# An RWKV and Hadamard FFN kernel on one core: the order of the next tokens' statistics and the next weights' loads in the first block's last product

## Chip, core and metric

The kernel runs on one core of a Trainium2 chip. The metric is the device time in microseconds from launch to end; several runs of each kernel are taken and their median is compared. One further execution was recorded by the hardware profiler; all start times below are counted from the first instruction of that recording.

## What is computed

The input `x` has 4 sequences of 2048 tokens with 512 channels, all in float32. After a layer norm without gain or bias, two branches are added to the input: an RWKV-v4 attention and a gated FFN with a Walsh-Hadamard transform of its hidden layer.

```python
xn = _layernorm(x, axis=-1)
# attention branch
shifted = jnp.pad(xn, ((0, 0), (1, 0), (0, 0)))[:, :-1]
xr, xk, xv = (mu * xn + (1.0 - mu) * shifted for mu in (mu_r, mu_k, mu_v))
r, k, v = xr @ Wr.T, xk @ Wk.T, xv @ Wv.T
attn = (sigmoid(r) * wkv_v4(k, v, wkv_w, wkv_u)) @ Wo.T     # a recurrence over the tokens
# FFN branch
hidden = fwht(silu(xn @ W1.T) * (xn @ W3.T))                # 2048 wide
out = x + attn + hidden @ W2.T
```

## The kernel before

The 8192 tokens are worked through in 8 blocks of `TB` = 1024, two blocks to a sequence. A block has these stages: the three projections to r, k and v; 16 products up (`up`, gate and linear weights together) with the recurrence woven in; and a last product, called down, in which the hidden layer and the recurrence's output are multiplied by the joined weights of `W2` (with the Hadamard transform folded in) and `Wo`. The products are Strassen-like: seven products of sums and differences ("forms") of quarters stand for eight. Forms of weights are made once, on POOL, in the block that uses them first (`seven_forms`, four additions), and then kept in DRAM (`part_w`, `down_w`, `deep_w`) for later blocks.

Block 0 does its down product in `down_whole` (line 636), one level deep: seven products of four pieces each. A piece is 320 KB of weights; it serves ten matmuls of 128x512. `pieces_w` is a ring of eight pieces. `Down.product` (line 613) first issues the load of the piece seven ahead and then its own matmuls, so the load stands in SyncE's queue at the place where the code reaches it, and it waits until the piece that had its slot has been used. Later blocks use `down` (line 727), with another hand-written order.

Work for the next block is spread into the down product by an object of the class `Chores` (line 931) and a function `next_parts` (line 1063):

- `chores.start()` copies the last column of the old tokens on DVE and issues the load of the next block's tokens by channel, 2 MB into `xnT`, on SyncE.
- `chores.statistics(n)` advances the generator `statistics` (line 163) by n steps. For eight groups of tokens, ACT sums over the channels (into `sums`); POOL makes `mean` of it; eight more ACT passes make the sums of squares; three POOL instructions make `rs` (the inverse deviation, and the mean times it). SyncE stores `rs` to `stat_d` in DRAM and loads it back to all partitions as `spread`, a part of the tile `v_sb`. In block 0 all 16 steps are issued at once. The token-major input of these passes, `x_tok`, lies in the tile `tf`; its load (`load_tokens`) is issued before the down product begins.
- `chores.tokens(n)` advances the normalizing on DVE (it reads `spread` and `xnT`) and the token forms.
- `next_parts()` issues the loads of the first two weight tiles of the next block, into the three-tile ring `ring_a` (tile name `part`). At the end of block 0, the first has its forms already and is loaded whole from `part_w` (896 KB). The second is the first of the projections' weights, used for the first time in block 1: it is loaded from `wpart` (512 KB), and `load_parts` (line 394) at once issues its four form additions on POOL.

All engines are wrapped in `InOrder`: each engine, and each engine's queue of DMA issues, keeps the order in which the code issues. All DMAs are issued on SyncE. So an instruction that waits on SyncE or POOL holds up whatever stands behind it on that engine. (The profile gives almost every instruction the line of this wrapper, L35; so instructions are told apart by the names of their tiles.)

In `down_whole`, product 0 (pieces 0 to 3 of 28) is issued first, then the differences of the right side for a later product, then the next block's work, and then product 1 with `c11`, which adds to the residual x11 and stores it; the loads of pieces 11 to 14 are issued in product 1.

Of the kernel before, what the change touches and what calls it, by code (L numbers as in the profile page):

```python
# [18 lines left out]
TP = TB // P  # L19
# [21 lines left out]
def tile_rwkv_attn_hadamard_ffn(  # L41
# [73 lines left out]
    def bank():  # L115
        turn[0] += 1
        return banks[(turn[0] - 1) % 8]
# [276 lines left out]
    def load_parts(i, n):  # L394
        t = ring_a.tile([P, 7, KH, P], F32, tag="a", name=f"part_{i}_{n}")
        if is_first(i, n):
            sp.dma_start(out=t[:, 0:4], in_=wpart[n])
            forms_in(t)
        else:
            sp.dma_start(out=t, in_=part_w[n])  # L400
        return t
# [179 lines left out]
    def parts_of(kh, half):  # L581

        return [quarter(kh, half, rh, cols) for rh in range(2) for cols in (lo, hi)]
# [4 lines left out]
    def differences(out, x0, x1):  # L588
        for o, p0, p1 in zip(out, x0, x1):
            difference(o, p0, p1)  # L590

    def add(slot, pt, cols=whole):
        dve.tensor_tensor(slot[:, cols], pt[:, cols], slot[:, cols], ALU.add)
# [42 lines left out]
    def down_whole(i, chores, next_parts):  # L636

        d = Down(i)
        y11, y12, y21, y22 = (parts_of(kh, half) for kh in range(2) for half in range(2))
        pa, pb, pc = ([bank() for _ in range(KH)] for _ in range(3))  # L640
        s5 = [small.tile([P, H], F32, tag="s5", name=f"s5_{i}_d{g}") for g in range(KH)]
        d.residual(x11, 0, 0)
        d.plain_product(0, pa, (0, 0), lambda g: act.copy(pb[g], pa[g]), True)
        differences(y11, y12, y11)
        chores.start()
        next_parts()
        chores.statistics(2 * TP)

        def c11(g):
            add(x11[g], pa[g])  # L650
            d.store(x11[g], 0, g, 0)

        d.plain_product(1, pa, (1, 0), c11)
        d.residual(x12, 0, 1)
        d.residual(x22, 1, 1)
        d.plain_product(4, pc, (0, 0), lambda g: act.copy(s5[g], pc[g]), True)
        differences(y12, y22, y12)
        for g in range(KH):
            add(x22[g], s5[g])
        chores.tokens(6)  # L660
        d.plain_product(6, pc, (1, 1), lambda g: None)
        differences(y22, y22, y11)
        d.plain_product(5, pb, (1, 1), lambda g: act.copy(u2_of[g], pb[g]))
        differences(y21, y21, y22)
        for g in range(KH):
            add(x12[g], pc[g])
            add(x12[g], u2_of[g])
            d.store(x12[g], 0, g, 1)
        d.residual(x21, 1, 0)
        chores.tokens(2)  # L670

        def c22(g):
            add(x22[g], pb[g])
            d.store(x22[g], 1, g, 1)

        d.plain_product(3, pb, (0, 1), c22)
        chores.tokens(4)
        chores.mix()

        def c21(g):  # L680
            add(x21[g], pb[g])
            d.store(x21[g], 1, g, 0)

        d.plain_product(2, pb, (1, 0), c21)
# [242 lines left out]
    def order_of(i):  # L927
        rkv, (first, *rest) = range(3 * KH), range(3 * KH, 3 * KH + NF)
        return [first, *rest] if i == 0 else [first, *rkv, *rest]
# [29 lines left out]
    for i in range(n_blocks):  # L959
# [46 lines left out]
        else:  # L1006


            def mix_chores(*kinds):
                for kind in kinds:  # L1010
                    mix_before(kind, 0)
                    for b in range(NB):
                        if b + 1 < NB:
                            mix_before(kind, b + 1)
                        mix_here(kind, b)
                        yield
                    yield from mix_forms(kind)
# [7 lines left out]
            chores, hooks = mix_chores(2, 0), [0]  # L1025
# [37 lines left out]
        def next_parts():  # L1063
            if not last:
                parts.extend(load_parts(i + 1, n) for n in order_of(i + 1)[:2])
# [3 lines left out]
        if i == 0:  # L1069
            down_whole(i, Chores(i + 1), next_parts)  # L1070
        else:
            down(i, Chores(i + 1), next_parts, last)
# [53 lines left out]
```

## Time and profile before

| | us |
|---|---|
| median of 3 runs (lowest, highest) | 3064.77 (3064.32, 3064.84) |
| the profiled execution's own time | 3062.49 |
| its span, first to last instruction | 3060.7 |
| TensorE (PE) busy in it | 3027.3 (99%) |
| VectorE (DVE) busy | 2471.0 (81%) |
| ScalarE (ACT) busy | 1014.1 (33%) |
| GpSimd (POOL) busy | 233.0 (8%) |

The mean granted TensorE clock was 0.997 of full speed, and the kernel moved 397.64 MB by DMA. Busy times overlap, since engines work beside each other, and ends of matmuls are modelled, so that a busy TensorE isn't always one at full rate. An arrow `<-` between two engines means that the left one waited for the right one; `out<-in` names the tiles of an instruction. PEld is the weight load on TensorE, SPq an issue of a DMA on SyncE.

The first block's down product stands between 310.21 us, where its first matmul starts, and 445.00 us, where the first matmul of block 1 starts. Seven more blocks follow in the span.

### The profile page before, as it was taken

The page shows a single profiled execution, that of the slowest core. Times are in us where ns is not written, and L with a number is a line of the kernel's source. Part 1 is how long each engine was busy: PE and PEld are TensorE (multiplying, and loading weights), DVE is VectorE, ACT ScalarE, POOL GpSimd, SP SyncE. Part 2 cuts the span into 40 slices and gives each one's busy share as a digit, 9 for nine tenths or more (in the row PEclk, how much of TensorE's full clock was granted, in tenths as well). Part 3 has the DMA queues.
Part 4 walks back from the last instruction along what each step waited for, and adds up shares of the span by engine and source line. Part 5 has one row for each costly group of instructions (what it writes and reads, how often), then busy time and mean ns, then how long its engine had stood idle before and what let it go on. Part 6 is the DMA issues. An engine that isn't in the chain of part 4 may idle for free.

```text
span 3060.7 us, 24403 instructions
## 1 busy us (share of the span) xinstructions
PE 3027.3 (99%) x8492; PEld 1615.3 (53%) x8492; DVE 2471.0 (81%) x2579; ACT 1014.1 (33%) x1822; POOL 233.0 (8%) x192
## 2 busy tenths in 40 slices
PE   8999899999999999999999999999999999999999
PEld 3444344446744476444764448544485444844458
DVE  5798548998878878888788888879798897988876
ACT  4233214333243332433234332333324333143321
POOL 3363002330000000000000000000000000000000
PEclk9999999999999999999999999999999999999999
DMA  4264424565522254222632226322352224522234
GB/s 174 74 200 172 173 69 146 202 216 190 177 75 82 90 211 141 73 84 78 230 134 72 76 102 223 125 73 72 147 190 107 83 72 164 180 97 84 72 119 146
DMA packets 136058, 397.64 MB, mean 130 GB/s; under 512 B 14336, under 2 KB 32768, under 8 KB 133760
## 3 DMA queue, kind: packets, MB, share of 16 engines
q1 hardware_dynamic: 135936, 396.09, 37.2%
q8 instruction: 68, 1.11, 0.1%
q14 instruction: 54, 0.44, 0.0%
HBM read 336.08 MB, written 59.96 MB: 129 GB/s over the span
## 4 chain that ended last, share of the span: by engine, by line
PE 86%; DVE 1%; DMA 1%; POOL 0%; ACT 0%; issue 0%; SPq 0%; DVEq 0%
PE bank L35 86%; DMA pieces_w<-deep_w 0%; DVE e1b L35 0%; POOL rs L35 0%; DVE right L35 0%; DMA pieces_w<-down_w 0%; DMA stat_d<-rs 0%; DVE sa L35 0%; DVE v_sb L35 0%; DVE e L35 0%; DVE bank L35 0%; DVE sb L35 0%; ACT tf L35 0%; SPq L35 0%; ACT s_d L35 0%
## 5 line engine op out<-in xcount | busy, mean ns | idle before, releaser
L35 PE MATMUL bank<-tf,part 128*128 128x512 f32 x2048 | 941.9, 592 | 0.0
L35 PE MATMUL bank<-right,pieces_w 128*128 128x256 f32 (+1 forms) x2928 | 792.5, 431 | 14.6 <-DMA pieces_w<-down_w 11.8
L35 ACT COPY bank<-bank 128x512 f32<-128x512 f32 (+1 forms) x638 | 337.1, 528 | 1413.7 <-PE bank L35 1377.5
L35 PE MATMUL bank<-xnT,part 128*128 128x512 f32 x1536 | 722.2, 593 | 1.2 <-DVE right L35 1.2
L35 PEld LDWEIGHTS bank<-right,pieces_w 128*128 128x128 f32 x2928 | 557.5, 191 | 242.9 <-issue 167.9
L35 PEld LDWEIGHTS bank<-tf,part 128*128 128x128 f32 x2048 | 389.6, 190 | 489.6 <-issue 461.8
L35 PEld LDWEIGHTS bank<-xnT,part 128*128 128x128 f32 x1536 | 292.0, 190 | 366.5 <-issue 358.9
L35 DVE TENSOR_TENSOR right<-right 128x1280 f32<-128x1280 f32 (+2 forms) x236 | 328.9, 1420 | 64.7 <-PE bank L35 63.7
L35 PE MATMUL bank<-right,part 128*128 128x512 f32 x840 | 369.6, 594 | 0.0
L35 DVE SCALAR_TENSOR_TENSOR right<-right,bank 128x512 f32<-128x512 f32 x256 | 174.7, 682 | 218.9 <-ACT right L35 218.6
L35 PEld LDWEIGHTS bank<-right,part 128*128 128x128 f32 x840 | 158.6, 190 | 203.0 <-issue 189.2
L35 ACT ACTIVATE right<-bank 128x512 f32<-128x512 f32 x308 | 183.8, 600 | 124.1 <-PE bank L35 105.9
L35 DVE RECIPROCAL e1b<-e1b 128x512 f32<-128x512 f32 x64 | 214.2, 3347 | 1.1
L35 DVE TENSOR_TENSOR bank<-bank,s 128x512 f32<-128x512 f32 x256 | 168.8, 691 | 37.3 <-ACT bank L35 23.7
L35 DVE TENSOR_TENSOR right<-right,bank 128x512 f32<-128x512 f32 x256 | 173.6, 678 | 11.5 <-PE bank L35 7.1
L35 POOL TENSOR_SCALAR mean<-sums 128x8 f32<-128x8 f32 x7 | 5.0, 715 | 1814.7 <-ACT tf L35 1462.7
L35 DVE SCALAR_TENSOR_TENSOR right<-xnT,vec,right 128x1024 f32<-128x1024 f32 x92 | 119.7, 1337 | 14.3 <-ACT right L35 14.3
L35 ACT COPY s<-bank 128x512 f32<-128x512 f32 x128 | 74.9, 585 | 144.9 <-PE bank L35 144.8
L35 POOL TENSOR_TENSOR part<-part 128x256 f32<-128x256 f32 x88 | 89.9, 1032 | 266.3 <-DMA part<-wpart 159.0
L35 ACT ACTIVATE right<-xnT,omm 128x1024 f32<-128x1024 f32 x92 | 100.3, 1143 | 12.3 <-PE bank L35 12.3
L35 PE MATMUL bank<-pieces_w,part 128*128 128x512 f32 x224 | 100.7, 592 | 0.0
L35 PE MATMUL bank<-k_sb,pieces_w 128*128 128x256 f32 x420 | 97.5, 379 | 0.0
(120 smaller groups left out, 2300.9 us busy)
## 6 DMA issues: line engine op xcount, KB each, us to landing
part<-part_w SPq DMA_DIRECT2D x148, 896.0 KB, 4.6
pieces_w<-deep_w SPq DMA_DIRECT2D x294, 320.0 KB, 3.1
pieces_w<-down_w SPq DMA_DIRECT2D x80, 320.0 KB, 5.4
part_w<-part SPq DMA_DIRECT2D x22, 896.0 KB, 6.1
tf<-x SPq DMA_DIRECT2D x7, 2048.0 KB, 7.9
xnT<-xT SPq DMA_DIRECT2D x7, 2048.0 KB, 10.0
deep_w<-pieces_w SPq DMA_DIRECT2D x6, 2240.0 KB, 8.1
v_sb<-xT SPq DMA_DIRECT2D x48, 256.0 KB, 8.1
```

The source lines that it names most:

```text
L35: return self.tc.keep_in_program_order(issue(*args, **kwargs))
```

## The change

In `down_whole` two lines change places:

```diff
         d.plain_product(0, pa, (0, 0), lambda g: act.copy(pb[g], pa[g]), True)
         differences(y11, y12, y11)
         chores.start()
+        chores.statistics(2 * TP)
         next_parts()
-        chores.statistics(2 * TP)
 
         def c11(g):
             add(x11[g], pa[g])
```

The statistics of the next block's tokens (16 ACT passes, four POOL instructions, the store of `rs` and the load of `spread`) are now issued ahead of the two weight loads and of the four form additions. The other blocks, which use `down`, are left as they were. What is computed stays the same.

## The prediction

> **What bounds the kernel now.** I read first the page's busy table and its costliest groups: TensorE is busy 3027.3 of 3060.7 us, at a mean granted clock of 0.997. Only time in which TensorE stands still or runs slowly can be won. TensorE's own waits are few, and the longest is one wait for a piece of the down weights:
>
> ```profile
> PE bank L35 <- DMA pieces_w<-down_w: 11.8, 1, 11.8
> PE bank L35 <- DMA right<-w: 9.9, 1, 9.9
> PE bank L35 <- ACT right L35: 3.9, 1, 3.9
> ```
>
> Columns: who waited for what, total us, times, longest. The timeline of TensorE puts it in the first block's last product, where the edit is; the table by stretches adds the clock (columns: busy us, matmuls, granted clock, DMA share, GB/s):
>
> ```profile
> 310.21 47.37 PE L35 MATMUL bank<-right,pieces_w 128*128 128x512 f32 x110
> 369.39 75.77 PE L35 MATMUL bank<-right,pieces_w 128*128 128x512 f32 x170 [11.81 <-DMA pieces_w<-down_w]
> 445.00 1.88 PE L35 MATMUL bank<-xnT,part 128*128 128x512 f32 x4
> ```
>
> ```profile
> 357.60:369.30 11.70, 0.00 (x0) 0.64 0.37 142
> 369.40:373.70 4.30, 4.30 (x5) 0.50 1.05 408
> ```
>
> See: 110 matmuls are 11 pieces of 10 (pieces 0 to 10), so what is late is piece 11; after the pause TensorE runs at half clock for a while. Why piece 11 is late is in SyncE's queue (start, issue time):
>
> ```profile
> 337.06 0.38 SPq L35 DMA_DIRECT2D xnT<-xT  x1
> 337.49 0.50 SPq L35 DMA_DIRECT2D part<-part_w  x1
> 338.04 0.42 SPq L35 DMA_DIRECT2D part<-wpart  x1
> 361.68 0.37 SPq L35 DMA_DIRECT2D stat_d<-rs  x1
> 363.24 0.32 SPq L35 DMA_DIRECT2D v_sb<-stat_d  x1
> 363.65 0.86 SPq L35 DMA_DIRECT2D pieces_w<-down_w  x2
> ```
>
> The queue stands for 23.1 us on the store of the statistics, and piece 11 is the first load behind it. POOL and ACT say what the statistics waited for:
>
> ```profile
> 348.03 5.33 POOL L35 TENSOR_TENSOR part<-part 128x256 f32<-128x256 f32 x4 [66.44 <-DMA part<-wpart]
> 353.33 0.24 POOL L35 TENSOR_SCALAR mean<-sums 128x8 f32<-128x8 f32 x1
> 359.43 0.20 POOL L35 TENSOR_SCALAR rs<-sums 128x8 f32<-128x8 f32 x1 [5.86 <-ACT tf L35]
> ```
>
> ```profile
> 332.88 0.19 ACT L35 ACTIVATION_READ_ACCUMULATOR tf<-tf 128x1 f32 x1
> 353.60 0.72 ACT L35 ACTIVATE tf<-tf,mean 128x512 f32<-128x512 f32 x1 [20.54 <-POOL mean L35]
> ```
>
> ACT's sums are done at 332.88+0.19 = 333.07. The mean on POOL stands in program order behind the four forms, which wait until 348.03 for their 512 KB from wpart. So ACT waits 20.54 us for a mean whose inputs were ready, and everything to piece 11 follows.
>
> **What the Trainium skill says.** "TensorE: Matmul & The Clock Gate" (Part 1, What's actually happening): after an idle window of about 3.4 us the clock falls to half and comes back after such a window of work. The trace agrees: clock 0.64 in the pause, 0.50 with 5 matmuls in the next 4.30 us. "SBUF — State Buffer" (Who interferes with whom): a VectorE instruction with two SBUF inputs blocks a GpSimd one that reads SBUF. The trace fits: the four forms took 718 to 1855 ns, beside VectorE's differences. "DMA: Bandwidth & Descriptors" (Queues, rings and completion order): each DMA engine takes descriptors in ring order. Here xnT landed 7.4 us after its issue, the two part loads 9.1 and 9.8 us: I treat bytes ahead in the queue as ahead in time.
>
> **The change, part by part.** Nothing is added or removed; two loads (896 and 512 KB) and four POOL forms move behind the statistics' instructions, on SyncE and on POOL. On ACT nothing changes place.
>
> POOL and ACT: the mean can start at 333.1. VectorE is then in differences (331.26 to 336.95), so instead of 0.24 us the mean may take 0.79 (median of the seven) or at most the 1.86 of a blocked form: I take 0.8, ready 333.9. The second pass of ACT, 353.60 to 359.35 = 5.75, then ends at 339.7. The three rs steps took 359.43 to 361.65 = 2.2; VectorE is idle from 337.6 to 344.7, so again 2.2 (bound: medians elsewhere, 0.85+2.91+1.46 = 5.2). The statistics' store is issued at 342.0 instead of 361.7.
>
> DMA: this tiny store took 1.54 us in an empty queue. Now the 2 MB of xnT, issued at 337.06, are ahead until about 343.6 to 344.5 (7.4 us when shared). I take landing at 345.0 (bounds 343.5 and, with the slow rs steps and the slow mean, 347.8). Then in the queue: the spread load (v_sb<-stat_d) at 345.0, the two part loads, piece 11 at 346.4. Before, piece 11 landed at 369.35, 6.1 us after the spread load was issued at 363.24. Now 1.44 MB of part loads are between; the DMA window 335 to 350 shows about 410 GB/s, so 3.5 us more: 345.0+6.1+3.5 = 354.6 (353.1 to 357.4).
>
> TensorE: a matmul comes every (47.37-0.59)/109 = 0.4292 us. Piece 11 is wanted at 310.21+110x0.4292 = 357.4. Forecast margin 2.8 us; at the worst bound, none, but then a stall of tenths and no clock loss. Pieces 12 to 14 follow 0.8 us apart, against 4.29 us each on TensorE. SyncE also stops on the landing of the eighth DMA before (it held a v_sb load until about 368.3, when the spread landed, and the first e load to 369.36, when piece 11 did); by that rule the residual x22 is issued near 354.7 and piece 15 near 356, wanted at 374.6.
>
> The sum, on the profiled execution: from 310.21 to 445.00 is 134.79 us for 280 matmuls, which at 0.4292 are 120.17. The loss is 14.62: 369.39-357.42 = 11.97 standing, and 75.61-170x0.4292 = 2.65 at half clock. I count both as gone.
>
> What is late next: VectorE. It adds s_d to x22 only when piece 11 is done (361.7+0.6), then six normalizing steps (7.27) to about 370.4, then the differences of y22, which can start when piece 14 is done, 374.6. That 4 us distance was there before as well (4.38 us of waiting for TensorE at 389.40). The moved loads are wanted at 445.0-14.6 = 430.4 and land near 353; the moved forms run near 354, where nobody waits. At 445.20 VectorE comes from a 7.89 us wait for TensorE and SyncE stores results just added, so later work starts from TensorE's time and shifts with it.
>
> The profiled execution took 3062.49 us (span 3060.7): 3047.9 after. It lies 2.3 us below the median of the timed runs, 3064.77; subtracting from the median gives 3050.2. About 0.2% (6 us) can be told from no change.
>
> **The rivals.** (1) A shorter stall remains, 3053 to 3060, say 3056: the part loads delay piece 11 past 357.4, for instance if the broadcast load and the part loads share bandwidth badly. A stall of 3.6 us would need 361; at over 3.4 us the clock loss of 2.65 is back. For it: 2.8 us is a small margin and 1.44 MB really are put ahead of the piece. Against: it needs 6.4 us beyond an estimate made from landings in this stretch.
>
> (2) The gain is given back: 3064.8. The chain of waits runs on VectorE from 571 to 603 and twice more through a statistics store (1127.50, 1500.24). Were one of these tied to a fixed time instead of to TensorE, it would eat up to 14.6. Against: the engines meet at 445.
>
> (3) Slower, 3069: the statistics' store isn't held by POOL's order but by something else that stays, so it still goes out near 361.7; then the part loads only stand ahead of piece 11: 0.92 us of issue and 3.5 us of bytes, +4.4. It decides if the store is issued later than about 361.7-4.4 = 357.3. Against: ACT names the mean, and the mean starts as the last form ends.
>
> That the change does nothing isn't likely, as each of the engines keeps program order.
>
> **How the numbers follow.** Forecast 0.88 (own range 3047 to 3053: the 2.3 us between profile and timed runs, and half clock varying by a window); rival 1 0.06, rival 2 0.03, rival 3 0.03. Range 3046.8 to 3053.8, which leaves rivals 1 to 3 out. Faster: 0.88 and most of rival 1, 0.93; same 0.04; slower 0.03.
>
> **What would show it.** The mean at 333 to 335 on POOL; ACT's second pass right behind; the statistics' store near 342, part loads after it; TensorE without a wait on pieces_w<-down_w and clock 1.00 from 310 to 430; the next block's first matmul near 430.4. Wrong, if TensorE still waits over 1 us there, if the store is past 350, or if a new wait appears between 374 and 640.

## The result and the profile after

| | before | changed |
|---|---|---|
| median of the runs timed together (4 each), us | 3064.81 | 3048.56 |
| lowest to highest | 3064.32 to 3066.58 | 3048.06 to 3049.55 |
| profiled execution, its own time | 3062.49 | 3048.46 |
| its span | 3060.7 | 3046.7 |

The ratio of the times is 0.9946, with a 95% interval of 0.9929 to 0.9964: the changed kernel is about 16 us faster, between 11 and 22. A second set of runs gave 3048.48 against 3064.74, ratio 0.9947 (0.9934 to 0.9961).

The longest of TensorE's waits in the changed kernel (who waited for what, total us, times, longest):

```profile
PE bank L35 <- DMA right<-w: 7.6, 1, 7.6
PE bank L35 <- ACT right L35: 3.9, 1, 3.9
PE bank L35 <- DVE v_sb L35: 2.5, 1, 2.5
```

The wait for `pieces_w<-down_w`, once the longest, is gone, and no new long one has come. TensorE's timeline of the stretch (start, length):

```profile
308.67 120.33 PE L35 MATMUL bank<-right,pieces_w 128*128 128x512 f32 x280
428.83 1.88 PE L35 MATMUL bank<-xnT,part 128*128 128x512 f32 x4
```

One unbroken row of 280 matmuls has taken the place of the rows of 110 and 170. From the first of them to the next block's first matmul it is 428.83-308.67 = 120.16 us, where it was 134.79. (The stretch begins 1.54 us earlier than in the profile of before. That arises ahead of the edited place and isn't part of the change: over all twelve profiles of this document the start varies from 308.46 to 310.77 us.) The clock, in the table by stretches (busy us, matmuls, granted clock, DMA share, GB/s):

```profile
310.20:357.20 47.00, 47.00 (x111) 1.00 0.61 229
357.20:361.50 4.30, 4.30 (x12) 1.00 1.07 406
361.50:420.00 58.50, 58.50 (x138) 1.00 0.25 78
```

Full clock throughout: the half clock after the pause went with the pause. How the piece came to be in time is told by SyncE's queue and POOL (timelines):

```profile
335.51 0.38 SPq L35 DMA_DIRECT2D xnT<-xT  x1
340.81 0.37 SPq L35 DMA_DIRECT2D stat_d<-rs  x1
343.15 0.33 SPq L35 DMA_DIRECT2D v_sb<-stat_d  x1
343.53 0.43 SPq L35 DMA_DIRECT2D part<-part_w  x1
344.01 0.42 SPq L35 DMA_DIRECT2D part<-wpart  x1
344.53 1.11 SPq L35 DMA_DIRECT2D pieces_w<-down_w  x2
```

```profile
331.61 1.08 POOL L35 TENSOR_SCALAR mean<-sums 128x8 f32<-128x8 f32 x1 [51.46 <-ACT tf L35]
338.56 0.20 POOL L35 TENSOR_SCALAR rs<-sums 128x8 f32<-128x8 f32 x1 [5.86 <-ACT tf L35]
338.84 1.67 POOL L35 TENSOR_TENSOR rs<-rs,neg_half 128x8 f32<-128x8 f32 x1
340.58 0.20 POOL L35 TENSOR_TENSOR rs<-mean,rs 128x8 f32<-128x8 f32 x1
351.69 3.01 POOL L35 TENSOR_TENSOR part<-part 128x256 f32<-128x256 f32 x4 [10.90 <-issue]
```

The mean starts as soon as ACT has the sums, not behind the forms. The store to `stat_d` goes out at 340.81 (361.68 before), and the queue moves on. Piece 11 is the first of the two pieces issued at 344.53. It landed 8.33 us later, at 352.86, and TensorE wanted it at 308.67+110x0.4292 = 355.88: 3.0 us to spare. The forms now run at 351.69, just behind the landing of wpart (351.56), with nobody waiting.

### The profile page after: what moved, and what is told of

Read it like the earlier page. It is cut to its first block, busy times and chain, and to the rows that moved or that the text cites. A ratio compares the mean times of both kernels' runs of the same rounds, so it can differ in the third digit from the quotient of the medians.

```text
span 3046.7 us, 24404 instructions
## 1 busy us (share of the span) xinstructions
PE 3027.2 (99%) x8492; PEld 1613.7 (53%) x8492; DVE 2468.0 (81%) x2579; ACT 1014.6 (33%) x1822; POOL 231.9 (8%) x192
## 4 chain that ended last, share of the span: by engine, by line
PE 95%; DVE 3%; DMA 1%; POOL 1%; ACT 0%; issue 0%; SPq 0%; POOLq 0%; ACTq 0%; DVEq 0%
PE bank L35 95%; DMA pieces_w<-deep_w 1%; DVE right L35 1%; DVE e1b L35 1%; POOL rs L35 1%; DVE e L35 0%; DVE xnT L35 0%; DMA stat_d<-rs 0%; DVE sb L35 0%; DVE sa L35 0%; DVE bank L35 0%; DVE v_sb L35 0%; DMA right<-w 0%; SPq L35 0%; ACT tf L35 0%
## 6 DMA issues: line engine op xcount, KB each, us to landing
deep_w<-pieces_w SPq DMA_DIRECT2D x6, 2240.0 KB, 10.3
```

## The experiments

The stretch of the profile from the first down matmul to the next block's first matmul is the sharpest measure here: in three profiles each it was 134.79, 135.10 and 135.13 us before, and 120.17, 120.17 and 120.17 after. Whole times scatter by several us (before, from 3060.04 to 3067.97 in 31 runs), so both are given. The runs come from three chips; each ratio is to runs of the kernel before taken with it (medians from 3064.74 to 3065.36).

| kernel | median us (lowest to highest, runs) | ratio to before (95%) | stretch us | piece 11 landed ahead of need, us |
|---|---|---|---|---|
| changed | 3048.48 (3045.5 to 3053.27, 5) | 0.9947 (0.9934 to 0.9961) | 120.17 | 3.0 |
| POOL's half only | 3049.11 (3048.16 to 3053.51, 5) | 0.9953 (0.9941 to 0.9966) | 120.17 | 2.9 |
| piece 11 first | 3060.27 (3056.68 to 3063.3, 21) | 0.9986 (0.998 to 0.9993) | 130.83 | (piece 12 late) |
| loads first | 3048.72 (3048.09 to 3054.43, 5) | 0.9954 (0.9941 to 0.9966) | 120.58 | -0.3 |
| loads last | 3048.75 (3047.23 to 3050.48, 5) | 0.9949 (0.9935 to 0.9962) | 120.17 | 6.2 |
| 1.05 MB more ahead | 3051.13 (3049.42 to 3052.88, 4) | 0.9958 (0.9944 to 0.9971) | 120.17 | 0.6 |
| 3.15 MB more ahead | 3056.49 (3054.97 to 3060.61, 11) | 0.9978 (0.9969 to 0.9987) | 125.86 | -4.1 |

**Which of the two orders mattered: POOL's half alone.** The loads stay ahead of the statistics on SyncE, and only the forms move on POOL.

```diff
             sp.dma_start(out=t[:, 0:4], in_=wpart[n])
-            forms_in(t)
+            if held:
+                held.append(t)
+            else:
+                forms_in(t)
...
         chores.start()
+        held.append(None)
         next_parts()
         chores.statistics(2 * TP)
+        forms_in(held[1])
+        held.clear()
```

> Half of the change: on POOL the four forms stand behind the statistics, on SyncE the two part loads stay ahead of the statistics' store. If the order on POOL is what held piece 11 (my theory): the mean starts near 332 to 333, the store is issued near 341 to 342 and lands behind the part loads near 346 to 347, piece 11 near 353, wanted at 356 to 357: no stall, about 3048.6 us, as the whole change. If it is the loads' place in SyncE's queue that counts (rival): the stall stays or shrinks only in part, 3055 to 3065.

Measured: 3049.11 us, stretch 120.17. The whole gain is there. Timeline of SyncE's queue in this kernel:

```profile
336.46 0.38 SPq L35 DMA_DIRECT2D xnT<-xT  x1
336.89 0.50 SPq L35 DMA_DIRECT2D part<-part_w  x1
337.44 0.42 SPq L35 DMA_DIRECT2D part<-wpart  x1
341.76 0.37 SPq L35 DMA_DIRECT2D stat_d<-rs  x1
347.58 0.32 SPq L35 DMA_DIRECT2D v_sb<-stat_d  x1
348.00 0.86 SPq L35 DMA_DIRECT2D pieces_w<-down_w  x2
```

See the 5.8 us between the 8 KB store and the load that waits for it; in the changed kernel it was 2.3. The store landed at 347.57, just behind wpart (347.38); in the changed kernel at 343.13, just behind xnT (342.95). So the store comes in the queue's turn, and whether the part loads stand ahead of the store or ahead of the piece is the same to piece 11: 2.9 and 3.0 us of margin. The order on POOL is the cause; once it is right, the order on SyncE makes no difference to the time. (SyncE's half alone isn't possible: wpart would stand behind the store, the store waits for the mean, and on POOL the mean would stand behind the forms, which wait for wpart.)

**Whether it was one late piece or a standing queue: piece 11 first.**

```diff
+        load_piece(i, 11)
         chores.start()
         next_parts()
         chores.statistics(2 * TP)
...
-            load_piece(self.i, self.u + 7)
+            if (self.i, self.u) != (0, 4):
+                load_piece(self.i, self.u + 7)
```

> The order of before, but the load of piece 11 alone is issued ahead of the next block's tokens, loads and statistics. Theory (the queue stands until 361.7, whatever is first behind it comes late): TensorE now waits for piece 12, wanted 4.29 us later, which lands when piece 11 did (about 369.4): a stall of 7.7 us and 2.65 us of half clock, 10.3 instead of 14.6, so about 3060.5 us. Rival (it was this one piece): no stall, about 3050.

Measured: 3060.27 us. TensorE's timeline:

```profile
308.75 51.66 PE L35 MATMUL bank<-right,pieces_w 128*128 128x512 f32 x120
368.20 71.54 PE L35 MATMUL bank<-right,pieces_w 128*128 128x512 f32 x160 [7.79 <-DMA pieces_w<-down_w]
```

The first row now has 120 matmuls, twelve pieces: the wait went on to piece 12. It is shorter by one piece's work, 7.79 us instead of 11.81 to 12.17. The stretch is 130.83-120.17 = 10.66 over the unstalled one (expected 10.3). The queue stands until the statistics are out; a single piece issued ahead of it only hands the wait to the next one.

**Whether the statistics must come first: the loads first.** Only `next_parts()` and `chores.start()` change places, so the part loads start before the 2 MB of tokens, and the forms still stand ahead of the mean. (In the kernel before, SyncE's queue stood for 13.4 us already ahead of the part loads: the tokens' load went out only at 337.06, behind VectorE's copy of the old last column, which ended at 337.03.)

```diff
+        next_parts()
         chores.start()
-        next_parts()
         chores.statistics(2 * TP)
```

> The order of before, but the two part loads with their forms are issued ahead of the 2 MB load of the next tokens too, so that they start near 324 instead of 337.5. Theory (the mean waits for the forms, and these only for the wpart load): wpart lands near 329, the four forms are done by about 332 to 336 beside VectorE's differences, the statistics' store goes out near 341 to 346, piece 11 lands near 350 to 354: no stall, about 3048.6 us, without the statistics being put first. Rival (POOL's forms must stand behind the statistics for it to help): a stall stays, over 3055 us.

Measured: 3048.72 us, as the changed kernel; but the stretch shows that this order stands at the edge. (The profiled execution was the slowest of the five, 3054.43 us: in block 1 TensorE waited 2.5 us for VectorE, and half clock followed.) POOL's timeline:

```profile
329.63 7.53 POOL L35 TENSOR_TENSOR part<-part 128x256 f32<-128x256 f32 x4 [48.49 <-DMA part<-wpart]
337.13 1.50 POOL L35 TENSOR_SCALAR mean<-sums 128x8 f32<-128x8 f32 x1
344.77 3.02 POOL L35 TENSOR_TENSOR rs<-rs,neg_half 128x8 f32<-128x8 f32 x1
347.87 1.26 POOL L35 TENSOR_TENSOR rs<-mean,rs 128x8 f32<-128x8 f32 x1
```

The part loads went out at 323.08 and 323.56, wpart landed at 329.47, as expected, and no longer holds the mean. But the forms now run beside VectorE's differences: 7.53 us for the four, where they took 3.01 with VectorE idle in the changed kernel. VectorE paid too: its four differences took 7.82 instead of 5.69 us. The rs steps then fell into the next differences (4.3 instead of 1.9 us for the last two). This is what "SBUF — State Buffer" (Who interferes with whom) describes, a VectorE instruction with two SBUF inputs against a GpSimd one that reads SBUF. The store went out at 349.16, later than the 341 to 346 expected, and piece 11 landed 0.3 us late. A version of the change, then, that needs no statistics first, but has no margin.

**What the margin is, and what it costs to lose it.** In the changed kernel further loads into idle tiles are put between the statistics and the part loads; they are work that the reference doesn't ask for. The larger dose:

```diff
         chores.statistics(2 * TP)
+        sp.dma_start(out=k_sb[:, 0:4, :], in_=xT[0 : 4 * P, ds(TB, TB)].rearrange("(b p) t -> p b t", p=P))
+        for s in (sa, sb):
+            sp.dma_start(out=s[:, 0:TB], in_=xT[0:P, ds(TB, TB)])
         next_parts()
```

> The changed kernel, with 3.15 MB of further loads (into tiles that nothing uses at that time) between the statistics and the part loads. It measures how far piece 11 is from being late. Its margin is 3.0 us in the changed kernel's trace (landed 352.86, wanted 355.88); 3.15 MB at about 410 GB/s are 7.7 us, so the piece lands near 360.5 and TensorE waits 4.6 us, and the half clock adds 2.65 more: about 3055.9 us. If the clock does not fall in so short a wait: 3053.2. If bytes ahead in the queue don't delay it (rival): 3048.6.

Measured: 3056.49 us. TensorE's timeline, and its table by stretches cut at the clock's steps (361.02 and 364.43 us):

```profile
310.10 47.37 PE L35 MATMUL bank<-right,pieces_w 128*128 128x512 f32 x110
361.41 74.71 PE L35 MATMUL bank<-right,pieces_w 128*128 128x512 f32 x170 [3.94 <-DMA pieces_w<-down_w]
```

```profile
357.61:361.02 3.41, 0.00 (x0) 1.00 1.00 371
361.02:364.43 3.41, 3.02 (x4) 0.50 1.04 405
```

The wait of the kernel before is back, 3.94 us long. The stretch grew by 125.86-120.17 = 5.7 us: 4.1 of standing, and 1.6 of reduced clock, not the 2.65 expected. The clock was at half from 361.02 to 364.43, for 3.02 us of work; in the kernel before it was so for 5.16 us of work, from 369.39 to 374.55. The median grew by 8.0 us; the stretch accounts for 5.7 of them, and the rest is within the scatter.

The smaller dose is the first line of the same edit with `k_sb[:, 0:2, :]`.

> The changed kernel, with 1.05 MB of further loads between the statistics and the part loads: 2.6 us at about 410 GB/s, less than the margin of 3.0 us. Theory: no stall or one of tenths, 3048.6 to 3049.1 us. If the margin is smaller than read from the trace: up to 3051.

Measured: 3051.13 us, over what was expected; two of the four runs took 3049.4 us and two 3052.8. Yet its profile has no wait for a piece: the stretch is 120.17, and piece 11 landed 0.6 us ahead of need (0.4 expected). With so little to spare, some executions may be late; that isn't shown, and the interval overlaps that of the changed kernel. This run doesn't decide.

**Nothing ahead of the piece: the loads last.** The statistics in their new place, `next_parts()` behind product 1.

```diff
         chores.start()
-        next_parts()
         chores.statistics(2 * TP)
...
         d.plain_product(1, pa, (1, 0), c11)
+        next_parts()
         d.residual(x12, 0, 1)
```

> The statistics in the place that the change gives them, and the two part loads with their forms behind the second product, so that nothing stands between the spread load and piece 11. By my arithmetic the part loads put 3.5 us ahead of piece 11: it should land 3 to 4 us earlier against its time than in the changed kernel (margin 6 to 7 us instead of 3.0), and since no stall was left, the time stays at 3048.5 us. A rival in which the margin is already worth something: under 3047.

Measured: 3048.75 us, stretch 120.17. Piece 11 landed 6.2 us ahead of need, so the part loads cost it 3.2 us in the changed kernel (3.5 in my arithmetic), and not using that room gains nothing. It isn't faster than the changed kernel, only safer. None of these orders beats it: with no stall left in the stretch there is nothing more here to win.

**Second and third profiles.**

> The changed kernel once more, for a second profile. In the first one the last ten matmuls took 4.08 us instead of 2.43 (half clock after a wait of 2.5 us for VectorE). If that is chance: it can be absent here, with a span up to 1.7 us shorter, and the median stays near 3048.6 us. If it belongs to the change: it is there again.

> The kernel before once more, for a second profile. Its first profiled execution lay 2.3 us under the median of the timed ones. If chance of the granted clock or of the first loads makes that: the stretch from the first down matmul to the next block is again 134.8 us within some tenths, and what differs is at the start or at the last matmuls. If the stall itself varies: the stretch differs by 1 us or more.

> A third profile of the kernel before. The stretch from the first down matmul to the next block is again 134.8 to 135.1 us. For the last ten matmuls: at full clock (2.4 us) if the phase of the clock's fall at the end goes with the kernel, as in the first two profiles; about 4 us if it is chance.

> A third profile of the changed kernel. The stretch from the first down matmul to the next block is again 120.2 us. For the last ten matmuls: about 4 us at half clock if that goes with the kernel, as in the first two profiles; 2.4 us if it is chance. The wait for VectorE in block 1, 0.5 and 2.8 us in the two profiles: different again, if it is chance.

Measured spans: changed 3046.7, 3051.5, 3044.5; before 3060.7, 3061.3, 3060.9. Cut into parts (us; block 1 is taken up to the 1481st matmul of the program, near 670 us in the kernel before and near 655 in the changed one):

| | to the first down matmul | stretch | then in block 1 | middle | from the tenth last matmul |
|---|---|---|---|---|---|
| before | 310.21, 310.77, 310.26 | 134.79, 135.10, 135.13 | 225.40, 224.57, 224.85 | 2384.86, 2385.37, 2385.23 | 5.45, 5.45, 5.46 |
| changed | 308.67, 310.60, 308.46 | 120.17, 120.17, 120.17 | 225.39, 228.11, 224.57 | 2385.34, 2385.47, 2384.45 | 7.11, 7.14, 6.88 |

The stretch carries the change, 14.6 to 15.0 us. The start and block 1 are chance: in the second profile of the changed kernel TensorE waited 2.8 us for VectorE in block 1 (followed by half clock), in the other two at most 0.5 us at a time, and the kernel before waits there too (1.25 us in its first profile). The last part isn't chance: the last ten matmuls ran at half clock in all three profiles of the changed kernel and in none of the kernel before. The experiments agree: half clock in all five with a stretch of 120.17 to 125.86 us, full clock in the one with 130.83. The last rows of TensorE's timeline, first profile of before, then of the changed kernel:

```profile
3055.25 2.43 PE L35 MATMUL bank<-right,pieces_w 128*128 128x256 f32 x10 [2.48 <-DVE v_sb L35]
```

```profile
3039.57 4.08 PE L35 MATMUL bank<-right,pieces_w 128*128 128x256 f32 x10 [2.47 <-DVE v_sb L35]
```

The wait ahead of them is the same; only the clock differs, and it takes 1.4 to 1.7 us of the gain back. Why the clock differs is told in the last section.

## Why the prediction was right

- **The cause.** The chain (forms wait for wpart, mean behind forms, ACT behind mean, store behind ACT, pieces behind the store) was confirmed from both ends: POOL's order alone gives all of the gain, and an earlier wpart load gives it as well. Rival 3 (the store held by something else) is refuted: counted from the first down matmul it went out at 32.1 us instead of 51.5.
- **The steps.** Counted from the first down matmul: the mean was forecast ready at 23.7 and was at 24.0 (it took 1.08 us beside VectorE, 0.8 assumed); the store's issue at 31.8, was 32.1; its landing at 34.8, was 34.5; piece 11 at 44.4, was 44.2; the margin 2.8, was 3.0. The stretch was forecast at 120.17 and measured as that.
- **Rival 1** (part loads push the piece too late) wasn't met. Its price in the forecast, 2.65 us of clock for a stall over 3.4 us, was too high for a short one: 1.6 after 3.94 us. After 7.79 us it was 2.7, hardly more than the 2.65 after 11.81 us. It comes to about half of the time that TensorE worked until the clock was back (3.02, 5.32 and 5.16 us).
- **Rival 2** (given back later): true to a tenth, in a place that it didn't name. VectorE's chain in block 1 and the two statistics stores shift with TensorE, but the clock at the end gives back 1.4 to 1.7.
- **The size.** 14.6 was forecast and the medians differ by 16.3. The stretch itself shows 14.6 to 15.0; the remaining 1.3 to 1.7 us, and the 1.4 to 1.7 that the end took, aren't traced to a place. The runs of the kernel before hint at the clock: of the 31, the 11 with a mean granted clock of 0.996 have a median of 3066.0 us, the 20 with 0.997 one of 3063.5, and all three profiles had 0.997. So some timed runs probably had more half clock than any profile here; no trace shows it. The interval, 11 to 22 us, holds the forecast, and the spans of the three profiles each differ by 13.4 on average, so timed runs and profiles don't agree to better than a few us here. With the clock's loss at the end the forecast's own sum would have been about 13 us; that the measured 16.3 came as near to 14.6 as it did is in part luck.

The step that the forecast left out is the clock at the end: it counted half clock only where a stall was removed, and didn't ask how a later, short wait would then lie to the clock's steps.

## What to carry to other kernels

When a load is late, look for what its issuing queue stood on, and follow that through the other engines' program order; here a 20 us hold of a tiny mean, behind four additions whose results no matmul used before block 1, some 90 us later, stopped all weight loads. Put small work that others wait for ahead of work that waits for a large load on the same engine. Then measure how many microseconds the rescued transfer has to spare, since orders with equal times had margins from -0.3 to 6.2 us.

## What was not expected of the hardware

- A wait of 2.5 us was enough to bring half clock, but only where nearly all of it lay in one clock window. In every one of the twelve profiles the steps of the clock lie whole multiples of 3.4133 us apart (first profile of the kernel before: 26.39, 360.89, 374.55 and 3060.84 us; the distances are 98, 4 and 787 times 3.4133), so the span can be cut into windows of that length. The last wait of the kernel before, and below it that of the changed kernel, by these windows:

```profile
3050.60:3054.01 3.41, 2.17 (x11) 1.00 0.16 61
3054.01:3057.43 3.42, 2.18 (x10) 1.00 0.56 208
```

```profile
3036.13:3039.54 3.41, 0.96 (x5) 1.00 0.40 154
3039.54:3042.96 3.42, 3.39 (x8) 0.50 0.32 115
```

In the kernel before the wait is split between two windows; in the changed one it lies but for 0.02 us in a single window, and the clock falls at that window's end. Over the twelve profiles, from 30 us on, each window at full clock in which TensorE stood still for 2.27 us or more was followed by half clock, and none with 1.62 us or less was; nothing lies between. "TensorE: Matmul & The Clock Gate" (Part 1, What's actually happening) speaks of an idle window of about 3.4 us and calls the window free-running. The length agrees, but the window need not be idle throughout: 2.27 of 3.41 us did it here.

Why it went with the kernel: in all twelve profiles the first down matmul came 283.1 to 284.5 us, 82.9 to 83.4 windows, after the first lasting rise to full clock. So the kernel kept nearly the same place in the windows although its start varied by 2 us. The 14.6 to 15.0 us that went are four windows and 1.0 to 1.3 us, and the last wait, which began 1.8 to 2.2 us into its window before, began 0.1 to 1.0 us into it after.

- The landings of SyncE's transfers were in the order of issue throughout this stretch, and an 8 KB store took 1.54 us in an empty queue, 2.32 when issued 5.3 us after a load of 2 MB, and 5.80 with 3.5 MB ahead, issued 4.3 us after the last of them.
- In this program SyncE also waited for the landing of the eighth transfer before: in the changed kernel the second residual load was issued at 351.63, with wpart landing at 351.56, and the two x22 loads at 352.88 and 353.67, with pieces landing at 352.86 and 353.66. It cost nothing here.
